# Cond's typed feed-forward layer by Strassen's scheme on eighths of the sorted batches, with attention cut into steps between its products

## The chip, the core and the metric

The kernel runs on one core of a Trainium2 chip. The time is the device time of one execution in microseconds (us), the median of several runs. The engines: TensorE (PE in the profile) multiplies matrices, VectorE (DVE), ScalarE (ACT) and GpSimd (POOL) work element by element, SyncE (SP) issues most of the transfers between DRAM and the on-chip memory (SBUF). Products land in PSUM, eight banks of 512 fp32 columns by 128 partitions.

## The reference, cut to what matters

The input x has 64 batches of 64 tokens with 256 features; `itok` gives each batch one of three types. In order:

```
# Cond: gated feed-forward, 256 -> 1024 -> 256, gelu(x Wi0) * (x Wi1) @ Wo
share  = ffn(x, sWi0, sWi1, sWo)                      # the same weights for all batches
expert = ffn(x, Wi0[type], Wi1[type], Wo[type])       # weights by the batch's type
w      = softmax(relu([expert[:,0], share[:,0]] @ g0) @ g1)
c      = expert * w[:,0] + share * w[:,1]
# attention: causal, 16 heads of 16, with biases
x      = x + attention(c)
# Cond2: two typed relu layers, three shared relu layers and a gate over them
# FFN: a router of three layers, 8 experts, top 2, with a capacity of 10 per batch of 64 tokens
x      = x + FFN(Cond2(x, type))
```

All of it is fp32. The change touches Cond's typed layer (`expert`) and the order in which the attention is laid beside other work.

## The kernel before

Tokens are kept with features on the partitions: `X` is [128, 2, 4352], two halves of the 256 features, the tokens sorted by type, with a spare block of 256 columns at the end. An "eighth" is 8 batches, 512 tokens (`NG`, `SB`); a "block" is 4 batches, 256 tokens (`GB`, `BT`). Every matmul goes through `mm` (L115, L116). An fp32 matmul is two instructions in the profile.

The work on TensorE is a list of items (class `Item`, L75): `first()` makes the hidden layer of one part, `second()` multiplies it down. `pipeline` (L373) lays them one after the other, so that `first` of the next item stands ahead of `second` of this one; functions hung on an item by `hook` (L383) run between the two. A scheduler then orders each engine's instructions by priority (the order written) and readiness, so instructions of neighbouring steps mix; `issue_after` holds some of them behind others.

- **Strassen items.** `strassen` (L207) makes a product of 2 by 2 blocks with seven products instead of eight. It works on weight blocks and on token blocks, of which some are sums of others (`BLOCKS`, L153). The products land in banks of the pool "ps" (`bank`, L105, four banks); ACT copies one out (L227), DVE adds the others up (L231, L238, L242, L246, L251). `layer` (L277) builds a feed-forward layer on an eighth from it: with two weight matrices (gated) ACT makes the gelu (L294) and DVE the product with it (L301); the sums of the hidden blocks are made on DVE and POOL (`token_sums`, L190). The down products add up in four more banks ("acc0", "acc1") over the items of the layer. The layers built so are Cond's shared layer (items named c), Cond2's shared layers (d) and Cond2's typed layer (t), and the router is made of the same scheme.
- **Weights of Strassen layers.** A half of a weight matrix with its sums is 7 KB per partition, 896 KB in all. For Cond2's typed layer, `sum_half` (L880) loads half a matrix, lets POOL make the sums (`sum_weights`, L177) and writes both to DRAM during the first stage; there are 16 such halves, with two buffers in turn. `send2` (L1035) fetches them by the type of the eighth.
- **Cond's typed layer.** `typed(0, m)` (L937) works without the scheme: sort (L544) pads each type to whole blocks, 18 blocks in nine steps of two. An item is a quarter of the 1024 hidden features for one block: four matmuls each for gate, linear part and down product. `send` (L904) fetches half matrices of 512 KB into a ring of six. The results are copied by ACT into a window (`win`, L1001) at columns known at run time, and shifted each eighth (`shift_win`, L1147).
- **Cond2's typed layer** works on fixed eighths of the sorted batches. An eighth is given its most frequent type; batches of another type in it (at most two such groups, found by `units`, L639) are done apart by `typed(1, 0)`, with two blocks, and picked out of a DRAM copy (`keep_typed`, `fetch_typed`, L1010 to L1023).
- **Attention.** `combine1` (L1167) makes the gate of an eighth in five steps; `attention` (L1187) gives queries and keys (two steps), scores and softmax of two batches (`weights`, L1232, four steps of two blocks), their mix (`mix`, L1264, four steps) and the projection. In a softmax block DVE adds the mask (L1249), takes the maximum (L1254), subtracts it (L1255), ACT takes the exponential (L1256), DVE adds up (L1258), inverts (L1259) and multiplies (L1260). The values are copied across partitions by SP (L1226) after POOL's L1223. A fixed plan (L1488) hangs these steps on the typed items from the third typed step on; what is left runs beside Cond2's first shared layer, two steps per item at first. The scores and mixes use the accumulation banks "acc1", except in the last eighth.
- **Trickle.** `tick` (L263), called within Strassen layers after every second product, runs one waiting function from a list, `between`.

Of the kernel before, what the change touches and what calls it, by code (L numbers as in the profile page):

```python
# [9 lines left out]
F32 = mybir.dt.float32  # L10
I32 = mybir.dt.int32
# [10 lines left out]
NBLK = NB // GB + NTYPE - 1  # L22
NSB = NB // (2 * GB)
NSTEP = NBLK // 2
# [28 lines left out]
AT_KB, AT_QT, AT_CT, AT_OT, AT_PR, AT_PRT, AT_VB, AT_VX, AT_VN, AT_PART, AT_GT, AT_G0 = (  # L53
    AT + n for n in (28, 44, 48, 52, 56, 64, 68, 72, 74, 76, 80, 84)
)

AT_SHARE = (AT, AT + 28, AT)
AT_HOPS2 = ((AT_RING, AT + 92), (AT + 60, AT + 74), (AT_RING, AT_RING + 14))
AT_XSUM2, AT_XSUM2F = (AT_RING + 14, AT + 88, AT + 88), AT + 102
AT_KEEP2 = ((AT_RING + 18, AT_XE), (AT + 92, AT + 96), (AT + 106, AT + 106))  # L60
AT_PARTS, AT_GW1, AT_X1 = AT + 92, AT + 104, AT_H + 4
AT_GS = (AT + 88, AT + 112)
# [21 lines left out]
def adaln_attn_ffn(ctx: ExitStack, tc: tile.TileContext, a: dict, out: bass.AP):  # L84
# [173 lines left out]
    def trickle(steps, n):  # L258


        between.extend([lambda: next(steps, None)] * n)

    def tick():  # L263
        if between:
            f = between.pop(0)
            if f:
                with behind_opening():
                    f()
# [8 lines left out]
    def layer(name, n, ups, down, blocks_of, hops, part, after, ahead=None, at_st=AT_ST, scale=None):  # L277
# [4 lines left out]
        def item(g):  # L282
            def first():
# [4 lines left out]
                gs = area(AT_G1, 4, 2, HB) if len(lhs) == 2 else None  # L288
# [19 lines left out]
                for i, f in enumerate(lhs):  # L308
                    to = (gate_out, gate_done) if gs is not None and i == 0 else (c_out, c_done)
                    steps = strassen(f"{name}_{g}{i}", f, lambda op, k: b[op][:, k, :], 1, 2, HB, *to, at_st)  # L310
                    for m, _ in enumerate(steps):
                        if m % 2:
                            tick()
# [130 lines left out]
    def counters():  # L444

        K.iota18 = iota("iota18", [P, NB], [[1, NB]])
        K.iota4 = iota("iota4", [P, NB // GB], [[GB, NB // GB]])
        t = iota("iota_sb", [1, NSTEP, 2], [[SB, NSTEP], [0, 2]])
        K.iota_sb = t.rearrange("o m b -> o (m b)")
# [33 lines left out]
    def attention_masks():  # L483
# [27 lines left out]

        K.bk4 = const.tile([P, DC, 4], F32, name="bk4")
# [31 lines left out]
    def sort():  # L544
        iota18, iota4, iota_sb, bvals = K.iota18, K.iota4, K.iota_sb, K.bvals
# [15 lines left out]
        full = tmp([P, NTYPE, NB // GB], "full")  # L561
        nc.vector.tensor_tensor(
            full,
            cnt.unsqueeze(2).to_broadcast([P, NTYPE, NB // GB]),
            iota4.unsqueeze(1).to_broadcast([P, NTYPE, NB // GB]),
            ALU.is_gt,
        )
        nblk = tmp([P, NTYPE], "nblk")
        nc.vector.tensor_reduce(nblk, full, AX.X, ALU.add)

        begin = tmp([P, NTYPE], "begin")
        first = tmp([P, NTYPE], "first")
        for t_, by in ((begin, nblk), (first, cnt)):
            nc.vector.memset(t_[:, 0:1], 0.0)
            for t in range(1, NTYPE):
                nc.vector.tensor_add(t_[:, t : t + 1], t_[:, t - 1 : t], by[:, t - 1 : t])

        K.btype = tmp([P, NBLK], "btype")
        nc.vector.tensor_scalar(K.btype, iota18[:, 0:NBLK], begin[:, 1:2], None, ALU.is_ge)
        for t in range(2, NTYPE):  # L580
            nc.vector.scalar_tensor_tensor(
                K.btype, iota18[:, 0:NBLK], begin[:, t : t + 1], K.btype, ALU.is_ge, ALU.add
            )

        shift = tmp([P, NTYPE], "shift")
        nc.vector.scalar_tensor_tensor(shift, begin, -float(GB), first, ALU.mult, ALU.add)
        yield
        place = tmp([P, NBLK], "place")
        part = tmp([P, NBLK], "place_part")
        nc.vector.tensor_scalar(place, iota18[:, 0:NBLK], float(GB), None, ALU.mult)  # L590
        for t in range(NTYPE):
            nc.vector.tensor_scalar(
                part, K.btype, float(t), shift[:, t : t + 1], ALU.is_equal, ALU.mult
            )
            nc.vector.tensor_add(place, place, part)
        nc.vector.tensor_scalar(place, place, float(NB), None, ALU.min)
        K.btype_i = const.tile([1, NBLK], I32, name="btype_i")
        nc.vector.tensor_copy(K.btype_i, K.btype[0:1, :])
        col = tmp([1, NBLK], "col")
        nc.vector.tensor_scalar(col, place[0:1, :], float(S), None, ALU.mult)  # L600
        yield
        K.col_i = const.tile([1, NBLK], I32, name="col_i")
        nc.vector.tensor_copy(K.col_i, col)

        woff = tmp([1, NBLK], "woff")
        nc.vector.tensor_scalar(woff, iota_sb, float(-SB), 0.0, ALU.add, ALU.max)
        nc.vector.tensor_sub(woff, col, woff)
        yield
        K.woff_i = const.tile([1, NBLK], I32, name="woff_i")
        nc.vector.tensor_copy(K.woff_i, woff)  # L610
# [191 lines left out]
    spillt = dram.tile([NB + NFIX * GB, P, DC * S], F32, name="spillt")  # L802
# [49 lines left out]
    for s in range(NSB):  # L852
# [4 lines left out]
            (lambda s=s: prepare_x(s + 1)) if s + 1 < NSB else None,  # L857
# [12 lines left out]
    hook(items[4], lambda: trickle(unit, 70))  # L870
# [24 lines left out]
    for i, v in enumerate(halves):  # L895
        hook(items[1 + i * 13 // 16], lambda v=v, at=AT_SUM[i % 2]: sum_half(*v, at))
# [7 lines left out]
    def send():  # L904

        if sent[0] == len(queue) or queue[sent[0]][0] > stage[0]:
            return
# [1005 lines left out]
```

## Time and profile before

| what | value |
|---|---|
| median of 3 runs | 2828.47 us (2828.14 to 2829.37) |
| profiled execution, its own time | 2827.92 us |
| its span, first to last instruction | 2826.2 us |
| granted TensorE clock, mean | 0.999 |
| instructions | 38,550 |
| DMA | 262.29 MB, mean 93 GB/s |

| stretch of the span | what runs |
|---|---|
| 0 to 322 us | Cond's shared layer, sort, half-weight sums |
| 322 to 404 us | typed layer, steps 0 and 1 |
| 404 to 887 us | typed layer, steps 2 to 8, with gates and attention |
| 887 to 1071 us | Cond2's first shared layer with the rest of the attention |
| 1071 to 2016 us | Cond2: shared and typed layers |
| 2016 to 2826 us | router and experts |

How to read the profile: the page gives busy time of each engine, then the span in 40 slices with a digit for the busy share in tenths. "Windows" give busy time and instruction counts of each engine in given stretches. A group of instructions is a line, engine, operation, output and input with its count, busy time, mean in ns, and the idle time before it with what ended that. Matmuls overlap in the pipeline, so their mean duration is longer than the distance from one start to the next. PEld is the loading of weights into TensorE. Names are of tiles: peg, pel and e are Cond's typed layer; p1c to p7c, sac and sbc its shared layer; the same with d and t in Cond2; pq, pk, pv, sc, ppT, ov and po attention; pha, pfa, plga and pgwa its gate.

### The profile page before, as it was taken

How to read it: one execution, taken by the hardware profiler on the slowest of the kernel's cores; microseconds unless marked ns; L12 is line 12 of the kernel's file. 1: busy time of each engine (PE TensorE's matmuls, PEld its weight loads, DVE VectorE, ACT ScalarE, POOL GpSimd, SP SyncE). 2: the span in 40 equal slices, each digit the busy share in tenths (PEclk: the TensorE clock that was granted, in tenths of full speed). 3: DMA queues.
4: the chain of work that ended last, by engine and by line, in shares of the span. 5: the costliest groups of instructions: out<-in, count | busy, mean ns of one | idle time of the engine just before them, and what ended most of it. 6: DMA issues, size and time to landing. Idle time of an engine off the chain costs nothing.

```text
span 2826.2 us, 38550 instructions
## 1 busy us (share of the span) xinstructions
PE 2796.3 (99%) x14073; PEld 2291.6 (81%) x14073; DVE 1504.4 (53%) x2732; ACT 841.0 (30%) x1517; POOL 887.3 (31%) x894
## 2 busy tenths in 40 slices
PE   8999999999999999999999999999999999999998
PEld 7888887777777778888888888888888888887776
DVE  7777416666666674543446666666543333333443
ACT  2111114444444332211222222222222222221333
POOL 4544201111122355521323322335413333224332
PEclk9999999999999999999999999999999999999999
DMA  3443454333341011422153444444300000013330
GB/s 111 149 131 119 153 181 125 112 111 112 112 131 46 33 47 62 151 85 71 71 190 117 137 142 139 136 136 136 107 15 6 7 6 6 8 34 85 91 99 1
DMA packets 221677, 262.29 MB, mean 93 GB/s; under 512 B 106456, under 2 KB 178992, under 8 KB 221360
## 3 DMA queue, kind: packets, MB, share of 16 engines
q1 hardware_dynamic: 205136, 224.62, 25.7%
q0 software_dynamic: 16128, 34.16, 3.7%
q8 instruction: 112, 1.84, 0.3%
q10 hardware_dynamic: 224, 1.05, 0.1%
q14 instruction: 77, 0.63, 0.1%
HBM read 197.79 MB, written 59.35 MB: 91 GB/s over the span
## 4 chain that ended last, share of the span: by engine, by line
PE 63%; issue 2%; DMA 2%; DVE 1%; ACT 0%; POOL 0%; POOLq 0%; SPq 0%; DVEq 0%; ACTq 0%
PE sad L116 6%; PE p1r L116 5%; PE p5r L116 5%; PE sbd L116 4%; PE sat L116 4%; PE po L116 4%; PE p5d L116 3%; PE p1d L116 3%; PE sbt L116 3%; PE p6r L116 2%; PE p7r L116 2%; PE p4r L116 2%; PE p5t L116 2%; PE p1t L116 2%; PE p7d L116 1%
## 5 line engine op out<-in xcount | busy, mean ns | idle before, releaser
L194 POOL TENSOR_TENSOR arena<-arena 128x512 f32<-128x512 f32 (+1 forms) x151 | 200.9, 1331 | 671.5 <-DVE arena L192 518.5
L195 POOL TENSOR_TENSOR arena<-arena 128x512 f32<-128x512 f32 (+1 forms) x151 | 180.1, 1193 | 19.1 <-DVE arena L193 15.2
L116 PE MATMUL sad<-arena 128*128 128x256 f32 x768 | 175.2, 379 | 0.0
L116 PE MATMUL e<-arena 128*128 128x256 f32 x704 | 173.1, 386 | 0.0
L116 PE MATMUL po<-arena 128*128 128x256 f32 (+1 forms) x704 | 169.8, 399 | 0.1
L1223 POOL TENSOR_TENSOR arena<-arena,vrest 128x256 f32<-128x256 f32 x32 | 24.8, 776 | 452.7 <-ACT arena L1220 452.7
L116 PEld LDWEIGHTS sad<-arena 128*128 128x128 f32 x768 | 144.0, 190 | 18.7
L116 PEld LDWEIGHTS po<-arena 128*128 128x128 f32 x704 | 132.7, 190 | 28.6 <-issue 11.2
L116 PEld LDWEIGHTS e<-arena 128*128 128x128 f32 x704 | 129.4, 190 | 28.6 <-issue 12.5
L116 PE MATMUL p5r<-arena 128*128 128x256 f32 x640 | 151.2, 383 | 0.0
L116 PE MATMUL p1r<-arena 128*128 128x256 f32 x640 | 150.1, 381 | 0.0
L116 PEld LDWEIGHTS p5r<-arena 128*128 128x128 f32 x640 | 119.2, 190 | 23.5 <-DVE arena L242 7.5
L116 PEld LDWEIGHTS p1r<-arena 128*128 128x128 f32 x640 | 119.7, 190 | 21.6 <-issue 5.9
L116 PE MATMUL peg<-arena 128*128 128x256 f32 x576 | 136.7, 380 | 0.0
L116 PE MATMUL pel<-arena 128*128 128x256 f32 x576 | 136.1, 379 | 0.0
L973 DVE TENSOR_TENSOR arena<-pel,arena 128x512 f32<-128x512 f32 x72 | 49.6, 689 | 159.4 <-PE pel L116 159.4
L116 PE MATMUL sbd<-arena 128*128 128x256 f32 x576 | 132.2, 379 | 0.0
L306 ACT ACTIVATE arena<-arena 128x512 f32<-128x512 f32 x144 | 90.7, 630 | 118.7 <-DVE arena L242 90.9
L1729 POOL DMA_INDIRECT xs<-arena,slot_i x64 | 62.6, 978 | 201.7 <-ACT arena L1725 108.8
L116 PEld LDWEIGHTS peg<-arena 128*128 128x128 f32 x576 | 108.9, 190 | 16.8 <-issue 2.3
L116 PEld LDWEIGHTS sbd<-arena 128*128 128x128 f32 x576 | 109.4, 190 | 14.9
L116 PEld LDWEIGHTS pel<-arena 128*128 128x128 f32 x576 | 109.4, 190 | 14.9
(411 smaller groups left out, 5916.3 us busy)
## 6 DMA issues: line engine op xcount, KB each, us to landing
arena<-in_L_cond_Wi SPq DMA_DIRECT2D x72, 512.0 KB
arena<-sums_i SPq DMA_DIRECT2D x32, 896.0 KB
arena<-sums_o SPq DMA_DIRECT2D x32, 896.0 KB
arena<-in_L_cond_Wo SPq DMA_DIRECT2D x36, 512.0 KB
arena<-in_L_ffn_eW SPq DMA_DIRECT2D x16, 1024.0 KB
spill<-arena SPq DMA_DIRECT2D x24, 512.0 KB
arena<-spill POOLq DMA_DIRECT2D x24, 512.0 KB, 4.7
arena<-arena SPq DMA_DIRECT2D x128, 64.0 KB
```

Source lines behind the costliest of these rows:

```text
L116: nc.tensor.matmul(o, lhsT=lhsT, rhs=rhs, start=start, stop=stop, skip_group_check=shared_bank)
L194: eng2.tensor_sub(t3, b22, b12)
L195: return r.ins, eng2.tensor_sub(t4, b21, t2).ins
L306: nc.scalar.activation(c_out(ij), src, AF.Relu)
L973: nc.vector.tensor_mul(h, hidden("i1", "pel"), g)
L1223: nc.gpsimd.tensor_mul(vx, vn, K.vrest.rearrange("p a b d -> p (a b d)"))
L1729: nc.gpsimd.indirect_dma_start(out=to.rearrange("e n w -> (e n) w"), out_offset=bass.IndirectOffsetOnAxis(ap=slot_i[:, n, i : i + 1], axis=0),
```

## The change

Cond's typed layer now follows the form of Cond2's. It works on the eight fixed eighths, each with its most frequent type, by a gated Strassen layer of two items (`typed1`); the batches of other types are done by one step of the old kind, `typed(0, 0)`, with two blocks, ahead of it. The sort no longer pads to blocks; the assignment of types (`units`) is trickled one item earlier. Window and shifts are gone: results go to DRAM, and an eighth fetches its eight batches by their place.

The 18 halves of Cond's three matrices for three types are summed in the first stage, in place of Cond2's 16. Cond2's 16 and the four halves of its first shared layer are summed while the typed part of Cond runs, one per item, in a single buffer. The first shared layer of Cond2 takes its weights from DRAM too.

```diff
+    halves = [
+        (a[f"L0_cond_W{w}"][e], w[0], g, sums1[w][g][e])
+        for g in range(2) for w in ("i0", "i1", "o") for e in range(NTYPE)
+    ]
     for i, v in enumerate(halves):
-        hook(items[1 + i * 13 // 16], lambda v=v, at=AT_SUM[i % 2]: sum_half(*v, at))
+        hook(items[1 + i * 12 // 18], lambda v=v, at=AT_SUM[i % 2]: sum_half(*v, at))
+    halves2 = [(a["L0_cond2_share_wi"][0], "i", g, sums_s["i"][g][0]) for g in range(2)]
...
+    queue1 = [("f", k, q, w) for k in range(NFIX) for q in range(2) for w in ("i0", "i1", "o")]
+    last = queue1.pop()
+    queue1 += in_order(0, 2 * NSB) + [("s", 1, "i"), ("s", 0, "o"), ("s", 1, "o")]
...
+        at = AT_RING1 + 7 * (sent1[0] % NRING1)
...
+            sync_dma(
+                area(at, 7 * 256), sums1[w[0]][g][bass.ds(types1[s], 1)].rearrange("e p n -> p (e n)")
+            )
+            ring1[n, w[0]] = half_blocks(w[0][0], at)
```

`NRING1` is 5. The layer itself, with two sends after each `first` and one after each `second`:

```diff
+    def typed1(s, ahead):
+        def ups(g):
+            return [lambda op, k, i, w=w: ring1[2 * s + g, w][op][:, k, i * P : (i + 1) * P] for w in ("i0", "i1")]
+        def after():
+            keep_typed(0, s * NG, NG)
+            while s and s - 1 not in summed:
+                tick()
+            fetch_typed(0, s)
+        its = layer(
+            f"e{s}", 2, ups, lambda g: lambda op, k: ring1[2 * s + g, "o"][op][:, k, :],
+            lambda: xblocks["e", s], AT_HOPSE, tp1, after, ahead, AT_STE, None, AT_G1E,
+        )
```

The plan of attention is gone. Gate and attention of an eighth are put into the list `between`, 16 steps, when the next eighth has begun, and `tick` takes one at a time; a step marked True is not taken at the first tick of a product. There is one more tick per gated item:

```diff
-                        if m % 2:
-                            tick()
+                        if m % 2 or (m == 6 and i + 1 < len(lhs)):
+                            tick(m > 1)
...
+        steps = [(lambda co=co: queries(co), False) for co in range(DC)]
+        steps += [(lambda: weights(0), True), (lambda: weights(1), True)]
+        for i in range(2, GB):
+            steps += [(lambda i=i: mix(i - 2), True), (lambda i=i: weights(i), True)]
+        return steps + [(lambda i=i: mix(i), True) for i in range(2, GB)] + [(whole, False)]
...
+    def begin_cond(s):
+        between.extend([(f, False) for f in combine1(s)] + attention(s))
...
+    starts = [10 + 2 * s for s in range(NSB)]
...
+    for s in range(NSB):
+        hook(items[n0 + starts[s]], lambda s=s: begin_cond(s))
```

The new part begins with the eight items of `typed(0, 0)`, so `begin_cond(0)` stands at the first item of the second eighth, and the last one at the first item of Cond2's shared layer.

Within attention, scores and mixes now always use the "ps" banks, and three kinds of steps change engine:

```diff
-                    nc.vector.tensor_scalar(
-                        qT[:, co, :], pq, K.bias["bq"][:, co : co + 1], HD**-0.5, ALU.add, ALU.mult
+                    nc.scalar.activation(
+                        qT[:, co, :], pq, AF.Identity, bias=K.bq[:, co : co + 1], scale=HD**-0.5
                     )
...
-                    if h % 2:
+                    if h == 3:
...
-            sc = [bank(f"sc{s}_{i}_{r}") for r in range(2)] if s == NSB - 1 else pair(f"sc{s}_{i}_", 1)
+            sc = [bank(f"sc{s}_{i}_{r}") for r in range(2)]
...
-                nc.vector.tensor_mul(pr, pr, sm.unsqueeze(2).to_broadcast([P, 8, S]))
+                nc.gpsimd.tensor_mul(pr, pr, sm.unsqueeze(2).to_broadcast([P, 8, S]))
```

The rest of the diff gives buffers new places in SBUF and carries the marks of the list through Cond2's and the router's steps.

## The prediction

> **What bounds the kernel now.** I read the page first, then busy time in windows of 50 us, then the groups of instructions of the attention stage, then what TensorE waited for.
>
> ```profile
> PE 2796.3 (99%) x14073; PEld 2291.6 (81%) x14073; DVE 1504.4 (53%) x2732; ACT 841.0 (30%) x1517; POOL 887.3 (31%) x894
> ...
> PEclk9999999999999999999999999999999999999999
> ```
>
> TensorE is busy all through at full clock; no other engine passes 53% on average. The chain of waits says the same (PE 63%, DVE 1%). So time is bought only with fewer TensorE instructions, and lost only where another engine lets TensorE wait. The stages differ, hence the windows (columns: stretch, length, then busy us and count of PE, PEld, DVE, ACT, POOL, then clock, DMA share, GB/s):
>
> ```profile
> 250.00:300.00 50.00, 50.00 (x232) 42.42 (x232) 34.62 (x56) 10.99 (x20) 23.05 (x28) 1.00 0.39 128
> 350.00:400.00 50.00, 50.00 (x233) 44.03 (x232) 6.92 (x10) 6.78 (x13) 0.00 (x0) 1.00 0.63 200
> ...
> 900.00:950.00 50.00, 47.81 (x362) 36.73 (x361) 40.63 (x73) 20.25 (x42) 23.47 (x23) 1.00 0.08 27
> ...
> 1000.00:1050.00 50.00, 47.58 (x314) 38.18 (x313) 39.05 (x72) 19.46 (x37) 25.98 (x26) 1.00 0.12 37
> ...
> 1300.00:1350.00 50.00, 50.00 (x226) 42.04 (x225) 22.90 (x37) 13.68 (x23) 17.69 (x16) 1.00 0.17 48
> ```
>
> 350 to 400 us is the typed layer as it is now, alone: 233 instructions in 50 us, 0.2146 us each, DVE nearly idle. 1300 to 1350 is Strassen's scheme alone (Cond2's shared layer): 226, 0.2212 us each, DVE half busy. 250 to 300 is the gated Strassen layer of Cond, DVE 69% busy, and TensorE has no idle time. From 900 to 950 and from 1000 to 1050 attention runs beside a Strassen layer: there DVE is busiest (81% and 78%) and TensorE loses 2.2 and 2.4 us. Two longer stretches give the typed stage with its attention, and the rest of the attention inside the shared layer:
>
> ```profile
> 321.50:887.00 565.50, 563.48 (x3495) 441.38 (x3494) 289.96 (x522) 228.97 (x380) 75.94 (x93) 1.00 0.40 122
> 887.00:1071.00 184.00, 178.91 (x1105) 139.12 (x1106) 132.09 (x225) 70.40 (x133) 81.14 (x80) 1.00 0.10 34
> ```
>
> **TensorE's own work.** One fp32 product of 256 columns is two instructions. The typed layer of Cond has 1,728 (the groups peg, pel and e: 576 each, e's other 128 belong to Cond2). It goes: 1,728 x 0.2146 = 370.8 us. In comes the part with fixed batches, two blocks of the former eighteen: 192 x 0.2146 = 41.2 us. And sixteen Strassen items, each two products up and one down of 14 matmuls, 84 instructions: 1,344 x 0.2212 = 297.3 us. Net: 192 instructions and 32.3 us less.
>
> Here a rule has to be weighed. By the rows' mean (379 ns for one 128x256 matmul) 192 instructions would be worth 73 us, since Strassen's and plain products have the same mean. The Trainium skill (Perfetto Trace Analysis, Identifying the Most-Contended Engine) warns that matmul busy time is no measure of the distance to the roofline, because matmuls overlap. The windows bear it out: 50 us hold 233 of them, not 132. I take the spacing, 32.3 us.
>
> **Attention beside Strassen.** Attention's matmuls stay as they are. One eighth of the batches costs 282 instructions. In the typed stage 3,495 - 1,728 = 1,767 are attention, 6.27 eighths, in 565.5 - 370.8 = 194.7 us: 31.1 us each. The other 1.73 eighths run inside the shared layer: of 1,105 instructions 488 are attention, about 77 transposes of the store at 0.109 us (spacing in the timeline), 540 Strassen: 184 - 119.4 - 8.4 = 56.2 us, 32.5 us each. Counted so, attention costs 1.4 us more per eighth beside Strassen, at 72% DVE. The change puts almost all eighths there, and one eighth is now much tighter:
>
> ```profile
> L1249 DVE TENSOR_TENSOR arena<-sc,causal 128x512 f32<-128x512 f32 x18 | 11.6, 686 | 9.7 <-PE sc L116 9.7
> L1254 DVE TENSOR_REDUCE mx<-arena 128x8 f32<-128x512 f32 x18 | 11.4, 676 | 0.0
> L1258 DVE TENSOR_REDUCE sm<-arena 128x8 f32<-128x512 f32 x18 | 11.6, 683 | 3.0 <-ACT arena L1256 2.5
> L1260 DVE TENSOR_TENSOR arena<-arena,sm 128x512 f32<-128x512 f32 x18 | 12.6, 742 | 0.0
> ```
>
> These are four of the five large DVE steps of a softmax block (name, count, busy us, mean ns, then idle time before), from 600 to 750 us. DVE per eighth after the change: 8 blocks x (0.69 + 0.68 + 0.68 + 0.68 + 0.20) = 23.4; keys 2 x 0.81 = 1.6; weighing and adding 6 x 0.69 = 4.1; output 2 x 0.75 = 1.5; gate 1.5: 32.1 us. The moves to ACT and POOL have already taken out 8 x 0.74 + 2 x 0.81 + 2 x 0.75 = 9.0 us. Strassen adds, by the gated layer's rows: 20 evictions x 0.69, 8 gate products x 0.71, 4 sums of about 0.8, 7 last evictions x 0.42: 25.6 us. Sum 57.7 us, against 168 x 0.2212 + 31.1 = 68.3 us of TensorE: 84%, for some 480 us on end. The gated layer runs at 69 to 78% without loss; at 78 to 81% with attention in the shared layer some 2.3 us in 50 were lost. The four "ps" PSUM banks now serve the products, the scores and the mixes alike, so a late DVE eviction holds a bank, and the next product waits for it:
>
> ```profile
> PE p1d L116 <- ACT arena L227: 2.4, 2, 2.0
> PE pgwa L116 <- DVE gwda L1128: 1.7, 1, 1.7
> ```
>
> Those are the two longest waits of TensorE between 890 and 1075 us: a late eviction on ACT and a gate step late on DVE. Bounds: nothing more (the gated layer's rows), and 7 us per eighth (DVE as the bound, below). I take 2 us, a little above 1.4 because of the higher load: 8 x 2 = 16 us.
>
> **The softmax product on POOL.** The last multiplication (0.74 us on DVE) goes to POOL, where a 128x512 step of two tensors takes 1.19 to 1.33 us (L195, L194): 8 x 1.26 = 10 us per eighth. POOL then has token sums 5, column sums 3, half-weight sums 9, values 9, this 10: 36 of 68 us. The rule against it: the Trainium skill (SBUF — State Buffer, Who interferes with whom) says that a DVE step with two SBUF inputs and a GpSimd step that reads SBUF shut each other out for the whole instruction. Taken literally, each of the 8 could hold DVE for up to 1.26 us, and the 5.9 us gained would be lost. The trace shows part of it: the weighing step L1143 takes 687 ns in the attention stage, where POOL is nearly idle, and 1170 ns in Cond2's typed stage, where it is busy for a third of the time; L193 takes 934 ns, its neighbour of the same shape 720. I add 3.3 us per eighth (four weighings 1.9, the rest on the subtractions), which puts DVE at 61 us, 89%; by the rule in full it would be 67.
>
> **Costed at nothing, or nearly.** The sort loses some 30 small DVE steps, 5.6 us by their durations, between 21 and 33 us, where DVE is the late engine; bounds 0 and -5, I take -1. Two more half sums in the first stage: 4.4 us of POOL each, hidden behind POOL's idle half; exposed they cost up to 9. The half weights: 896 KB each, three per item of 18 us without attention, 149 GB/s, beside up to 78 for the new sums; 200 GB/s ran at 0.63 of the DMA engines, and five buffers give 1.7 items of lead. On SP, behind a sum's load that waits for the only AT_SUM2 buffer (stores land in 3.9 us), stand the weights of later items, the batch fetches and the value copies; uncovered, 4 us for each of 20. ACT: the table loads (1.28 us, some 6 per eighth) rise to about 10, 42 of 68 us busy in all. Window shifts on ACT, the first shared layer's sums on POOL and its 2 MB load at the end go; they hid behind TensorE.
>
> **Sum.** The profiled execution took 2827.9 us (span 2826.2 and 1.7 around it): - 32.3 + 16 - 1 = 2810.6. The median of the runs is 0.5 above it: 2811 us.
>
> **Rivals.**
> - No new waits: if the scheduled order hides all as in the gated layer, 2828.4 - 33.3 = 2795. For it: no idle time at 78% DVE. Against: the two windows at 81%. Chance 0.14.
> - The forecast, 0 to 4 us per eighth, 2797 to 2827: 0.48.
> - DVE becomes the bound from the second eighth to the first shared eighth. If it gets no busier than the 81% of its best window, 61 us of work need 75 us: 6.9 us over TensorE's 68.3, seven times, 48 us: 2843, slower. It decides from 4.2 us per eighth, where the 33.3 us are used up. For it: a softmax block is 5.8 us of DVE beside 2.3 us of TensorE, and three can follow closely; against: DVE's steps overlap a little (in the timeline the next one starts up to 0.07 us before the last has ended), and TensorE's order can be filled from the other stream. Chance 0.27.
> - Weights late through SP: 16 items x 3.9 us = 62 on top of the forecast: 2873. Chance 0.06.
> - Anything better or worse than these: 0.05. That the count does not fall is excluded by the code.
>
> **How the numbers follow.** Within 0.2%, 2822.8 to 2834.1, a measurement can't tell it from no change. Faster: 0.14 + 0.40 of the forecast's 0.48 + 0.02 = 0.56. Same: 0.08 + 0.05 of the DVE case = 0.13. Slower: 0.31. The range leaves out half of the first rival and the worst tenth: 2795 to 2856.
>
> **What would show it.** PE count 13,881. From the end of the fixed part (near 360 us) each eighth should take 70 us. Right: TensorE idle 1 to 3 us in 50, its longest waits on DVE evictions (L231 to L251, the causal add). Wrong towards DVE: windows with DVE above 42 of 50 us and under 46 of PE. Wrong towards DMA: waits of products on "sums". No idle at all would mean that attention mixes freely.

## The result and the profile after

The changed kernel takes 2938.02 us, the median of 6 runs (2928.5 to 2943.36), beside 2828.69 us before: 1.0383 times as long, 95% interval 1.0366 to 1.0399. The forecast was 2811, its range 2795 to 2856: wrong in sign. The profiled execution took 2936.8 us (span 2935.1), 108.9 more than that of before, at a mean TensorE clock of 0.981 (0.999 before).

Page of the changed kernel, busy time of the engines and granted clock:

```profile
PE 2810.6 (96%) x13881; PEld 2266.6 (77%) x13881; DVE 1589.3 (54%) x2861; ACT 848.3 (29%) x1529; POOL 1097.1 (37%) x1121
...
PEclk9999998999899999999999999999999999999999
```

TensorE has the 13,881 instructions that were counted on, and is busy for longer with 192 fewer, at a lower mean clock. The next view places this: windows of the changed kernel, with columns as in the prediction.

```profile
250.00:300.00 50.00, 50.00 (x233) 42.55 (x232) 37.72 (x74) 11.80 (x19) 23.39 (x28) 1.00 0.38 115
350.00:400.00 50.00, 43.71 (x186) 36.33 (x186) 23.16 (x32) 9.36 (x16) 18.67 (x23) 0.93 0.74 257
400.00:450.00 50.00, 36.26 (x166) 30.52 (x164) 29.64 (x42) 7.47 (x13) 23.05 (x28) 0.91 0.67 225
500.00:550.00 50.00, 38.38 (x283) 28.67 (x284) 28.45 (x49) 18.84 (x32) 24.62 (x27) 0.86 0.40 129
550.00:600.00 50.00, 47.21 (x233) 32.04 (x233) 34.57 (x66) 25.31 (x36) 17.26 (x21) 1.00 0.35 111
700.00:750.00 50.00, 41.91 (x219) 28.35 (x218) 28.51 (x54) 16.33 (x28) 14.59 (x14) 0.93 0.19 62
800.00:850.00 50.00, 44.10 (x188) 28.52 (x188) 26.27 (x50) 17.07 (x27) 6.29 (x7) 0.84 0.29 86
...
350.00:1150.00 800.00, 694.67 (x4102) 500.43 (x4102) 495.16 (x858) 292.86 (x501) 341.90 (x372) 0.93 0.39 125
```

250 to 300 us, the first stage with its two more half sums, is untouched. From 350 to 900 us TensorE idles 6 to 14 us in each 50, and the clock falls as well; only the window from 550 to 600 us is nearly undisturbed. All the other engines have room: over these windows DVE is busy 23 to 37 of 50 us.

The same stretch of the kernel before:

```profile
350.00:1100.00 750.00, 742.89 (x4605) 578.45 (x4604) 429.62 (x757) 303.62 (x521) 168.11 (x182) 1.00 0.32 98
```

Both stretches cover the typed layer, the attention and the first products behind them. TensorE was idle 7.1 us before and 105.3 after: 98 us more. A product that both kernels share, the first one of Cond2's typed part, starts at 1244.3 us before and at 1354.0 after, 109.7 later; so the whole loss lies ahead of it. The sum: 32 less work, 3 saved in the opening (9.9 us idle up to 350 us instead of 12.5), 98 more idle, and 45 left over for the clock. The record of the clock bears this out by itself. Between 350 and 1150 us it stands at half in 16 pieces, 106 us in all. 17 of them fall into one long wait, and half of the other 89 is 44 us (a little less, since short waits lie in them too).

What TensorE waited for in the changed kernel (in total, times, longest, in us):

```profile
PE ppT L1307 <- POOL arena L1295: 25.2, 11, 4.1
PE pha L119 <- DMA arena<-spillt: 21.6, 1, 21.6
PE sae L119 <- DMA arena<-sums_o: 16.2, 6, 6.1
PE pq L119 <- DVE arena L1209: 9.3, 5, 2.4
PE ov L119 <- DMA arena<-arena: 5.9, 4, 2.8
```

The top two are a step of attention that waits for the step before it, and a gate that waits for its input through SP. The third is Strassen's down product that waits for its weights. None of the five is a product that waits for an eviction. By what ended them, the 105 us of idle time are 51 us in which steps of attention and gate waited for one another, 44 in which TensorE waited for transfers of weights and of the gate's input, and 10 in which products waited for DVE, ACT or POOL. Of the 89 us at half clock, 44 followed waits of the first kind, 37 waits for transfers, and 7 a mixed cluster.

How waits become lost clock is seen, for that cluster, in TensorE's timeline of the changed kernel (start, duration, instruction, idle time before it with its releaser):

```profile
498.34 0.63 PE L1307 MATMUL ppT<-ident,arena 128*128 128x128 f32 x4 [0.36 <-DVE arena L1284]
499.98 0.64 PE L119 MATMUL ov<-arena 128*32 128x64 f32 x16 [1.02 <-ACT arena L1312]
502.70 2.07 PE L119 MATMUL sae<-arena 128*128 128x256 f32 x4 [2.08 <-DVE arena L350]
504.57 1.91 PE L119 MATMUL p1e<-arena 128*128 128x256 f32 x4
...
510.16 1.03 PE L119 MATMUL p5e<-arena 128*128 128x256 f32 x4
```

These are three waits of 0.4 to 2.1 us in a row; then four matmuls of 256 columns take 2.07 and 1.91 us, and 1.03 again from 510. The clock record has half speed from 502.0 to 508.9. This is the only such cluster. Of the other 15 pieces, six set in at a wait longer than 3.4 us, seven at a wait of 1.7 to 2.5 us, and two at one or two waits of 2.3 to 3.3.

### The profile page after: what moved, and what is told of

Read it like the earlier page. It is cut to its first block, busy times and chain, and to the rows that moved or that the text cites. A ratio compares the mean times of both kernels' runs of the same rounds, so it can differ in the third digit from the quotient of the medians.

```text
span 2935.1 us, 38791 instructions
## 1 busy us (share of the span) xinstructions
PE 2810.6 (96%) x13881; PEld 2266.6 (77%) x13881; DVE 1589.3 (54%) x2861; ACT 848.3 (29%) x1529; POOL 1097.1 (37%) x1121
## 4 chain that ended last, share of the span: by engine, by line
PE 81%; DVE 5%; DMA 5%; issue 4%; POOL 3%; SPq 2%; ACT 1%; POOLq 0%; DVEq 0%; ACTq 0%
PE sad L119 5%; PE p5r L119 5%; PE p1r L119 5%; PE po L119 4%; PE sbd L119 4%; PE sat L119 4%; PE p5d L119 3%; PE p1d L119 3%; PE sbt L119 3%; PE p4r L119 2%; PE p6r L119 2%; PE p7r L119 2%; PE p5t L119 2%; PE p1t L119 2%; PE p5c L119 2%
## 5 line engine op out<-in xcount | busy, mean ns | idle before, releaser
L197 POOL TENSOR_TENSOR arena<-arena 128x512 f32<-128x512 f32 (+1 forms) x175 | 235.4, 1345 | 794.2 <-DVE arena L195 641.7
L198 POOL TENSOR_TENSOR arena<-arena 128x512 f32<-128x512 f32 (+1 forms) x175 | 205.7, 1176 | 37.3 <-PE p4e L119 15.4
L119 PEld LDWEIGHTS p1r<-arena 128*128 128x128 f32 x640 | 119.7, 190 | 21.6 <-issue 5.9
L188 POOL TENSOR_TENSOR arena<-arena 128x256 f32<-128x256 f32 (+1 forms) x53 | 49.1, 927 | 211.1 <-DMA arena<-in_L_cond_share_wi 49.2
L195 DVE TENSOR_TENSOR arena<-arena 128x512 f32<-128x512 f32 (+2 forms) x127 | 92.8, 731 | 55.3 <-ACT arena L310 30.5
L119 PEld LDWEIGHTS sbd<-arena 128*128 128x128 f32 x576 | 109.5, 191 | 16.2 <-issue 1.5
L119 PE MATMUL sat<-arena 128*128 128x256 f32 x512 | 120.9, 380 | 0.0
L196 DVE TENSOR_TENSOR arena<-arena 128x512 f32<-128x512 f32 (+2 forms) x127 | 109.7, 863 | 3.3
L230 ACT COPY arena<-p1d 128x512 f32<-128x512 f32 x48 | 28.1, 586 | 275.9 <-PE p1d L119 267.0
L1890 POOL DMA_INDIRECT out<-arena,rows_i x40 | 62.0, 1550 | 120.5 <-ACT arena L1889 59.5
L119 PEld LDWEIGHTS sat<-arena 128*128 128x128 f32 x512 | 96.7, 190 | 13.1
L119 PE MATMUL p1d<-arena 128*128 128x256 f32 x384 | 103.4, 392 | 0.2 <-ACT arena L230 0.2
```

The source lines that it names most:

```text
L119: nc.tensor.matmul(o, lhsT=lhsT, rhs=rhs, start=start, stop=stop, skip_group_check=shared_bank)
L188: eng.tensor_add(s1, a21, a22)
L195: eng.tensor_sub(t1, b12, b11)
L196: r = eng.tensor_sub(t2, b22, t1)
L197: eng2.tensor_sub(t3, b22, b12)
L198: return r.ins, eng2.tensor_sub(t4, b21, t2).ins
```

## The experiments

Where no number of runs is given, a time is of one run; the kernel before took between 2826.4 and 2831.3 us in its own runs beside them. The changed kernel alone spread from 2928 to 2943, so a difference of up to 15 us between single runs says little by itself. "Of 750" is TensorE's busy time from 350 to 1100 us, with the clock of that stretch.

The theories at the start were **S**, SP's single half-sum buffer (Q in the expectation); **P**, the softmax product on POOL; **D**, DVE as the bound (the prediction's rival; the expectations use the letter also for any limit in throughput, of POOL or of the PSUM banks); **L**, the distance between attention's dependent steps. **O** came later: the attention steps are ordered behind evictions.

**Edits of single suspects.** Three half-sum buffers instead of one, for the first nine sums:

```diff
-        hook(items[n0 + 2 + i], lambda v=v: sum_half(*v, AT_SUM2))
+        hook(items[n0 + 2 + i], lambda v=v, at=(AT_SUM2, 111, 118)[i % 3] if i < 9 else AT_SUM2: sum_half(*v, at))
```

> Edit: the first nine half sums of the second set use three buffers in turn (two lie in the place that the keys of the attention take later) instead of one; nothing else. Theory Q (SP waits for the one buffer's store every 12.5 us, and the fetches of weights and batches stand behind it): the waits for spillt (21.6 us), sums_o (16.2 us) and in_L_cond_Wi (4.2 us) and most of the half-clock time between 350 and 540 us go: 2870 to 2895 us. Rival D (DVE, or POOL's softmax product, is what holds the stage up): 2925 to 2940 us, the waits move to another name.

2919.44 us, 18 to 19 less than the changed kernel and less than half of the gain that S expected. This is SP's queue in the changed kernel (start, duration of issue, transfer):

```profile
417.61 0.92 SPq L126 DMA_DIRECT2D arena<-in_L_cond_expert_wi  x2
418.77 0.82 SPq L126 DMA_DIRECT2D arena<-sums_o  x1
428.93 0.89 SPq L126 DMA_DIRECT2D arena<-in_L_cond_expert_wo  x2
...
442.75 0.90 SPq L126 DMA_DIRECT2D arena<-in_L_cond_expert_wo  x2
444.50 11.28 SPq L126 DMA_DIRECT2D arena<-spillt  x8
```

Each load of a half (in_L_cond_expert) waits until the sums before it are stored, so they go out 11 to 14 us apart, and the gate's input (spillt) stands behind them. With three buffers the gate's wait fell from 21.6 to 3.0 us and its first matmul came at 440.6 instead of 457.9. The DMA engines then moved 338 GB/s at a share of 0.94 from 350 to 400 us. Waits of the kernel with three buffers, of which this edit touches only the last:

```profile
PE ppT L1307 <- POOL arena L1295: 25.3, 12, 3.8
...
PE sae L119 <- DMA arena<-sums_o: 15.8, 6, 6.4
...
PE pha L119 <- DMA arena<-spillt: 3.0, 1, 3.0
```

S holds, at 18 us. But SP was held up by more than this buffer, and three buffers do not touch the rest: the down products' weights (sums_o) come as late as before. SP's own waits in the changed kernel, the longest in total, and a part of its queue with the down product that follows on TensorE:

```profile
SPq L126 <- DVE arena L1209: 168.9, 7, 33.3
...
651.12 10.16 SPq L126 DMA_DIRECT2D arena<-spill  x8
661.88 0.38 SPq L126 DMA_DIRECT2D arena<-sums_o  x1
...
666.81 2.08 PE L119 MATMUL sae<-arena 128*128 128x256 f32 x4 [3.26 <-DMA arena<-sums_o]
```

L1209 is the gate's last step, which frees the place of the shared layer's batches; it ended at 651.0 us. SP had issued nothing since 617, then issued the eight loads of the next batches, and only then the weights. So a late gate also makes the weights late, by way of SP. In every run with the changed kernel's order of steps SP waits 152 to 172 us for L1209 and the down products 9 to 22 us for their weights (the two runs without attention apart); in every run with one of the two other orders below, SP waits 12 to 13 us and the down products not at all.

Then the product back on DVE:

```diff
-                nc.gpsimd.tensor_mul(pr, pr, sm.unsqueeze(2).to_broadcast([P, 8, S]))
+                nc.vector.tensor_mul(pr, pr, sm.unsqueeze(2).to_broadcast([P, 8, S]))
```

> Edit: the softmax's last product back on DVE, the rest as in the changed kernel. Theory P (the product on POOL comes late because POOL stands behind half sums and token sums): the waits of ppT for POOL (25.2 us) go with their half-clock time: 2895 to 2915 us. Rival D (DVE is the bound of the mixed stage, as the slower case of the forecast had it): 6 us more of DVE per eighth, 2940 us or more.

2929.99: 8 us less, within the spread. The 25.2 us of waiting for POOL's product became 5.6 us for DVE's, but the mixes now waited 11.1 us for POOL's masking of the values (L1262). P falls as a cause by itself: the wait moved. Both edits together:

> Edit: three buffers and the product on DVE together. If theories Q and P are both right and the losses are in different places, the two gains add up: 2830 to 2865 us. If DVE is the bound (rival D): 2900 us or more, with DVE above 42 of 50 us in the mixed stage.

2912.61, with 670.06 of 750. The time is in D's branch, but DVE stood at 28 to 42 of 50 us, above 42 in one window alone (42.4), so D's mark was not met.

**Attention left out.** First only attention's steps, with the gates kept (`between.extend([(f, False) for f in combine1(s)])`, on both edits):

> Edit: as both_edits, and the attention's own steps (queries to projection) are left out, so that x is not added to; the gate of Cond stays. If the loss lies in attention beside the Strassen layer, the layer alone runs as the gated shared layer does, 0.2155 to 0.2212 us per matmul with no idle time after its first eighth: 8 eighths of 38 us, and the whole takes 2555 to 2580 us (2828 less 33 less 8 times 29 to 31 us, the attention's price in the kernel before). If the layer itself waits for weights or batches even with free queues: over 2610 us.

2657.12, with the clock at 0.90 in places; but here the gate follows its own fetch so closely that it waited 51.8 us for it, in 8 waits. The run says nothing of Strassen alone. Hence without gates too:

```diff
-            while s and s - 1 not in summed:
-                tick()
...
-        between.extend([(f, False) for f in combine1(s)] + attention(s))
+        x1_done.add(s)
```

> Edit: three buffers; Cond's gate and the whole attention are left out, the results of the typed layer are still written to DRAM and fetched, nothing waits for them. All theories of mixing: the new layer alone runs at the rate of the shared Strassen layers, 0.2155 to 0.2212 us per matmul, no idle time after its first eighth: 2535 to 2565 us (2828 less 33 less 8 x 31). If the half weights from DRAM come late by themselves: sae and p1e wait for sums, 2580 us or more.

2564.81, at the upper end of what was expected. Windows of that kernel:

```profile
400.00:450.00 50.00, 50.00 (x229) 42.58 (x228) 31.37 (x51) 9.16 (x16) 21.64 (x23) 1.00 0.72 246
...
550.00:600.00 50.00, 50.00 (x230) 42.54 (x228) 30.40 (x49) 10.94 (x19) 19.38 (x21) 1.00 0.72 253
```

From 400 to 650 us there is no idle time and the clock is full, with 229 to 230 instructions in 50 us, DVE at 30 to 35 us and 231 to 278 GB/s. So the layer by itself delivers its gain, and the DMA traffic does not disturb it once SP is not held up. Two places lost: from 350 to 400 us PE was busy 43.88 at a clock of 0.90, where the part with fixed batches waits for its weights, and after the layer, from 650 to 700, it was busy 42.69, with a wait of 6.8 us at the first product of Cond2's shared layer, whose releaser the profile does not name.

**The order of the steps.** In the changed kernel all 16 steps of an eighth come in one sequence, so a step is followed by the one that needs its result a tick later (68.3 us for 16 steps, some 4.3 us). The plan of before laid the tail of one eighth's attention between the gate steps of the next. That order in the list, with the same work (one more call at the end puts the last tail in):

```diff
+        g = [(f, False) for f in combine1(s)] if s < NSB else []
+        q = attention(s) if s < NSB else []
+        m0, w2, m1, w3, m2, m3, o = tails.pop() if s else [None] * 7
+        order = (g[0:1], m0, w2, g[1:2], m1, w3, g[2:3], m2, g[3:4], m3, g[4:5], o, q[0:4])
+        for f in order:
+            between.extend(f if isinstance(f, list) else [f] if f else [])
+        if s < NSB:
+            tails.append(q[4:])
...
-    for s in range(NSB):
-        hook(items[n0 + starts[s]], lambda s=s: begin_cond(s))
+    for s in range(NSB + 1):
+        hook(items[n0 + 10 + 2 * s], lambda s=s: begin_cond(s))
```

> Edit: on top of both_edits (2913 us) the sixteen steps are put into the list in the old plan's order, the gate of an eighth between the last softmax blocks and mixes of the eighth before; same steps, same number of ticks. Theory L (the steps of one eighth follow each other too closely, so TensorE waits for the chain softmax to mix, gate to weighing to query, and its clock halves after such waits): the waits of ov, ppT, pq and plga go down by two thirds and with them most half-clock time: 2840 to 2870 us. Rival D (throughput of DVE, POOL or the PSUM banks beside Strassen): 2900 to 2920 us, the waits only change their names.

2870.7, on both edits: 42 less than without it, just above L's expectation. On three buffers alone, with the product on POOL:

> Edit: as overlapped_order, but the softmax's last product on POOL as in the changed kernel. Theory L: with more distance POOL's delay is covered too: within 10 us of overlapped_order, either way. Rival (POOL's delay is the cause by itself): 20 us or more slower than overlapped_order, with ppT waiting for POOL again.

2854.99: 64 less than three_buffers, the largest effect found, from order alone. L had expected at most 10 between this run and overlapped_order, the rival 20 or more the other way. Windows of this kernel:

```profile
600.00:650.00 50.00, 46.27 (x270) 31.44 (x262) 38.23 (x69) 24.14 (x38) 16.70 (x20) 1.00 0.34 99
...
800.00:850.00 50.00, 47.40 (x350) 35.54 (x349) 39.75 (x74) 22.61 (x39) 26.19 (x28) 1.00 0.54 183
...
350.00:1100.00 750.00, 699.32 (x4274) 515.50 (x4273) 510.28 (x885) 294.93 (x514) 353.40 (x384) 0.98 0.42 135
```

DVE is busier than in the changed kernel, and TensorE idles less: the opposite of what D says. The mean clock of the stretch rose from 0.93 to 0.98. Its longest waits:

```profile
PE pha L119 <- DMA arena<-spillt: 11.6, 5, 2.9
PE p7e L119 <- DVE arena L234: 9.1, 5, 2.3
...
PE ppT L1307 <- POOL arena L1295: 2.9, 1, 2.9
```

The wait for POOL's product fell from 25.3 us to 2.9 with the product still on POOL. It was the distance, not the engine. In this order POOL looks even like the better place for it, by 16 us against overlapped_order, one run each. Part of the 64 us came by way of SP: its wait for L1209 fell to 13.2 us, and with it went the down products' 15.8 us of waiting for weights and some 24 us of half clock behind them (worth 12), 28 us in all. A wait of the gate for its input took some of it back (11.6 us in place of 3.0).

The test from the other side is the kernel before with its plan closed up: two steps per item, eighths not overlapped.

```diff
-            (0, "g0"), (1, "g1"), (2, "g2"), (3, "g3"), (3, "g4"), (4, "q0"), (5, "q1"), (6, "w0"),
+            (0, "g0"), (0, "g1"), (1, "g2"), (1, "g3"), (2, "g4"), (2, "q0"), (3, "q1"), (3, "w0"),
```

> Edit: the kernel before, with its plan of attention changed only in order: two steps per typed item in the new kernel's sequence, without overlap of neighbouring eighths. There is no Strassen layer beside them, DVE is about half busy. Theory L: it loses too, 2860 to 2920 us, with waits of ppT, ov, pq and plga and half-clock stretches. Rival D (the loss needs Strassen's load on DVE and banks): 2825 to 2840 us.

2834.88, 4 to 6 more: L's expectation was missed, and the rival's met, by which the loss needs Strassen's load on DVE and the banks beside it. A window of that kernel:

```profile
650.00:700.00 50.00, 49.26 (x374) 36.17 (x373) 34.04 (x60) 27.24 (x46) 9.37 (x12) 1.00 0.35 103
```

Close steps beside the plain layer cost next to nothing. L must be narrowed: it is close steps beside the new Strassen layer that cost so much. What in that layer makes them costly, this run does not show. A finer interleaving, with neighbours in the chain further apart still by my count:

```diff
-        order = (g[0:1], m0, w2, g[1:2], m1, w3, g[2:3], m2, g[3:4], m3, g[4:5], o, q[0:4])
+        order = (m0, g[0:1], w2, g[1:2], m1, w3, g[2:4], m2, g[4:5], q[0:1], m3, o, q[1:4])
```

> Edit: on top of overlapped_pool (2855 us) the steps are fitted to the ticks of one eighth: the gate's first step one tick later, its weighing the tenth step, so that none has to be forced out before the fetch of the next eighth, and the first query before the last mix. Theory L (distance in time between dependent steps): waits of pha for spillt (11.6 us) and of sae (3.9 us) go: 2830 to 2845 us. Rival D (DVE is what TensorE waits for): the same 2855 us within 7, with p7e waiting for DVE as before.

2888.95: 34 more than overlapped_pool, a miss. Its waits show where it went: mixes for ACT (11.9 us) and for the values (11.5), queries for the weighed tokens (10.9), the gate for its own previous step (10.0). The query stands right behind the gate's last step, and two gate steps stand side by side. So it seems to be the distance of each single pair that counts, not the look of the whole.

**When the half sums run.** Only beside Strassen items, one buffer, in overlapped_order (`items[n0 + 8 + i * 14 // 20]`):

> Edit: as overlapped_order, but the second set of half sums starts only with the Strassen items (one buffer, 20 halves over 14 items) instead of in the part with fixed batches with three buffers. If the transfers of the first 100 us of the stage (338 to 351 GB/s, share 0.94) make the weights late (sae waits for sums_o, pel for in_L_cond_Wi, half clock at 358 and 440 us): 10 to 20 us faster than overlapped_order. If these waits come from the order on SP: the same or slower, since SP again waits for the one buffer.

2875.24, no gain.

**Is DVE the bound, or the chain's length?** The row's maximum and its subtraction left out of the softmax, in the changed kernel (two DVE steps of 128x512 per block less):

```diff
-                nc.vector.tensor_reduce(mx, pr, AX.X, ALU.max)
-                nc.vector.tensor_sub(pr, pr, mx.unsqueeze(2).to_broadcast([P, 8, S]))
```

> Edit: the changed kernel, but the softmax leaves out the row maximum and its subtraction (two of five large DVE steps of each block, 1.36 us of 5.8); order, buffers and engines as in the changed kernel. Theory D+L (the chain of DVE steps from the scores to the mix is too long for the work beside it): 2937 falls to 2880 to 2905 us, ppT waits for POOL less. If SP's order alone makes the loss: 2925 us or more.

2898.46, 40 less. A window of it:

```profile
650.00:700.00 50.00, 43.56 (x339) 30.52 (x340) 25.96 (x42) 22.83 (x38) 29.55 (x36) 0.97 0.58 192
```

DVE is half idle and TensorE still loses 6 us in 50. So D falls as a bound by DVE's throughput. That what the two steps gave back was length, some 1.6 us in each block's chain, is argued from the waits: POOL's product was waited for 10.6 us instead of 25.2, the gate's last step 5.3 instead of 9.3, and the weights longer than before (22.0). The same edit on exact_ticks, and then with the half sums spread over 17 items from the fifth on (`items[n0 + 5 + i * 17 // 20]`, three buffers for six):

> Edit: exact_ticks and no_max together (row maximum left out). If the remaining loss is DVE's load and chain: 2800 to 2825 us, below the kernel before, since 32 us of TensorE's work are gone. If the loss is in the transfers of the first 100 us and in the small matmuls' own rate: 2825 to 2845 us.

> Edit: as exact_no_max, and the second set of half sums starts three items later and is spread over 17 items (three buffers for the first six). If the transfers at 0.9 of the DMA engines between 350 and 450 us are what makes pel and sae wait there: 5 to 15 us faster than exact_no_max. If they wait for SP's order: no change or slower.

2876.47, far above both expectations, with 21.6 us in which mixes waited for the copied values; and 2870.98, 5 less, at the low end of what was expected and within the spread.

**Are the steps held up by their place in the order?** The steps of the list are issued behind the last eviction; here gate and attention are freed of that:

```diff
-                with behind_opening():
+                with nullcontext() if f in loose else behind_opening():
```

> Edit: the changed kernel, but the steps of gate and attention are no longer ordered behind the layer's last evictions and token sums on DVE and POOL (the old plan's steps were not either). Theory O (these edges put the softmax behind waits of the layer, so that TensorE waits for it): 2937 falls to 2870 to 2905 us. Theory L (distance in time alone): within 10 us of 2937.

> Edit: overlapped_pool (2855 us) with the steps not ordered behind evictions. Theory O: 2815 to 2840 us. Theory L: within 7 us of 2855.

> Edit: overlapped_unbound, and the softmax leaves out the row maximum and its subtraction. If DVE's load still costs (p7e waited 9 us for DVE in overlapped_pool): 10 to 25 us below overlapped_unbound. If distance and order are all: within 7 us of it.

2942.25 in the changed kernel (4 more), 2861.5 in overlapped_pool (6 to 7 more), and 2823.61 with the maximum left out as well (38 less than that, more than either branch gave). O falls for the softmax as it is; the next run bears on it once more.

**A version that beats both?** In several runs, the better order without the maximum, and the same edit in the kernel before:

> Edit: overlapped_pool (2855 us) and the softmax leaves out the row maximum and its subtraction; three buffers, old order of steps, product on POOL, steps ordered behind evictions as in the changed kernel. If DVE's chain is what was left, as overlapped_unbound_no_max (2824 us) says: 2810 to 2826 us, faster than the kernel before. If the edges behind evictions matter only with a light DVE: 2826 to 2840 us.

> Edit: the kernel before, and the softmax leaves out the row maximum and its subtraction. Its TensorE waits 2 us in the whole typed stage, so there is nothing to gain: 2825 to 2830 us, the same as before. If the steps on DVE cost something there too: 2815 to 2824 us.

overlapped_no_max: 2830.69 us (13 runs, 2826.51 to 2835.16), ratio 1.0006, interval 0.9998 to 1.0014. before_no_max: 2820.15 us (5 runs, 2817.29 to 2820.23), ratio 0.9962, interval 0.9948 to 0.9975, beside 2829.33 of the kernel before. Without the maximum the softmax has the same value on paper but no guard against overflow. Only this second kernel beats the kernel before clear of noise, by 9 us, and it has no Strassen in Cond's typed layer; with the same softmax the Strassen version is 10.5 us behind it. Its first expectation, no change, was missed; the other, 2815 to 2824 if DVE's steps cost something there too, was met. For overlapped_no_max the second branch was met: the order behind evictions matters with a light DVE. The same kernel freed of it took 2823.61, 7 us less and below all 13 runs, but in one run, so this remnant of O is not settled.

## Why the prediction was wrong, point by point

**TensorE's own work, 32.3 us less: right.** The count is exact, and layer_alone shows the spacing (50 / 229.5 = 0.218 us) in windows without idle time.

**Attention beside Strassen: the step that failed.** The prediction put it as "I take 2 us, a little above 1.4 because of the higher load: 8 x 2 = 16 us", bounded by 0 and 7 us per eighth. The stretch brought 98 us more idle and some 45 of half clock, 143 us, 18 per eighth. By the waits and the half clock that followed them, steps of attention and gate that waited for one another make about 73 of it (51 idle, 22 of half clock), 9 us per eighth in place of 2 and above the bound of 7; transfers make most of the rest and are taken up below. The price of 1.4 was taken from eighths whose steps stood in the old plan's order. The change kept the steps and threw that order away, and I costed the steps' loads (DVE 57.7 of 68.3 us) and never the time between one and the next, though the diff shows the new sequence. A chain of score, five DVE steps, exponential and product has to fit into the distance to the step that uses it; where it does not, TensorE waits, as the rows of ppT show. The order alone is worth 42 to 64 us, the part by way of SP included; a shorter chain 40 us in the changed kernel and 24 (2854.99 to 2830.69) in the better order.

**DVE as the bound, 2843: right in sign, wrong in mechanism.** Of its own two marks, PE under 46 of 50 came true in most windows, and DVE above 42 never did in the changed kernel. The mark towards DMA, waits of products on "sums", came true as well (16.2 us in six waits). The 5.8 us of DVE that this rival gives a softmax block are those of a step of two blocks; the sum for an eighth (8 x 2.93) is not touched by it.

**The softmax product on POOL: counted as load, needed as latency.** I asked what 1.26 us costs POOL and DVE (it took 1.04 in the median). What it cost was 25 us of TensorE at the end of the chain, until the order moved its reader away. The interference was taken as partial; the trace shows it whole where steps meet, but they met seldom. 37 of the 64 subtractions overlap a POOL step by more than 0.2 us. Some took their usual 0.68 us, and then POOL's step was the longer one (1.25 for 0.72 at 704.2 us); others were held up themselves, most to 1.2 us, five to between 2.0 and 4.3, one of these under five POOL steps in a row (1017.5 us). That agrees with the rule in full, and raised the mean of the subtraction over all 64 from 772 to 996 ns. The weighings took 685 ns because none of them met a POOL step. On DVE this cost some 2.5 us per eighth against its usual time, less than the 3.3 taken.

**"Costed at nothing": partly wrong.** This is the second step that failed. SP's queue was named, at 4 us for each of 20 or nothing, and the sum put nothing; the rival of late weights had 62 us and a chance of 0.06. Waits for transfers came to some 63 us in the changed kernel (44 idle, 19 of half clock). The half-sum buffer made one wait of 21.6 us, of a gate and not of a product, and three buffers gave 18 us back. The down products' weights made 16.2 us, with 14 of half clock: they stood behind batch loads that waited for the late gate, so this part belongs to the order of the steps as well. The weights of the part with fixed batches made 6.3, and about as much is left in the better orders. So the rival's size was nearly right by luck: it had 16 items late by 3.9 us each.

**A clock of 1.00 was assumed without a word.** The rows of before had one sign of it, which I passed over: waits of 1.7 and 0.4 us at 92 to 94 us, then a piece of half speed of 3.4 us.

```profile
50.00:100.00 50.00, 47.89 (x213) 40.03 (x212) 37.21 (x51) 10.50 (x18) 17.11 (x20) 0.97 0.37 108
```

The Trainium skill (TensorE: Matmul & The Clock Gate, Part 1) says that the clock halves after an idle window of about 3.4 us, counted free-running, and returns after a busy one. The pieces here are 3.4, 6.8 or longer multiples, as it says. But ten of the 16 set in at waits shorter than that window, seven of them at 1.7 to 2.5 us. Taken literally the rule would have charged only the six longer waits, some 17 of the 44 us.

**The opening, -1:** about -3.

**What stays open.** Why close steps cost 5 us beside the plain layer and far more beside Strassen's was not separated. Two candidates are only argued: products, scores and mixes now share four banks, so that a late step keeps a product out (in the changed kernel products waited about 10 us of the 105 for DVE, ACT or POOL, so little of it shows as such waits); and Strassen's products need DVE and ACT themselves, so less independent work is at hand. A third is part of it: the new layer gets its weights through a queue that the gate can hold up (16.2 us of waits), and in the kernel before with its plan closed up TensorE waited for no weights from 340 us on. The 26 us by which overlapped_pool is still above before, though it has 32 less work, are split only by its waits. That the half clock follows from the waits is seen in their order in time and in its rise to 0.98 and 0.99 with better orders; it was not varied alone.

## What to carry to other kernels

When a change re-orders steps, write down for each pair of dependent steps how far apart they stand on TensorE and how long the chain between them is, before adding up any engine's load: with DVE at 52% TensorE lost 6 us in 50 here, and with DVE at 80% it lost 3. The same holds for steps that free a buffer: here the gate's last step released SP, and the weights stood behind it. An operation moved off a busy engine is latency first, load second. Waits cost more than their sum once the clock follows them (105 us idle, some 44 more for the clock), and a load that waits for its buffer holds up everything behind it in its queue, whoever that is for.

## What the runs showed of the hardware that I had not expected

- Half clock at single short waits: 7 of 16 pieces in the changed kernel set in at one wait of 1.7 to 2.5 us, and all 16, 106 us, cost some 44 us.
- An engine with fewer operations need not free TensorE: with DVE at 26 of 50 us (no_max, 650 to 700 us) TensorE idled 6.4, with DVE at 37 in the same window of the changed kernel 5.6.
- Where a DVE step with two inputs in SBUF met POOL's steps, one of the two was held up: a subtraction of 0.68 us took up to 4.26 (changed kernel, 1017.5 us).
- The kernel before gained 9 us from two DVE steps less per block though TensorE waited only 7.1 us from 350 to 1100 us: 2.3 were left, and it did 4,637 instructions there instead of 4,605. The rest of the 9 us is not placed.
